# Second attention scores in two single PSUM banks, and layer 0's expert pieces only in turns with values

## The chip, the cores and the metric

The kernel runs on one core of a Trainium2 chip. The metric is the device time of one execution in microseconds (us); three runs of the kernel before are given by their median and their range. The profile is of one further execution of the same program on the chip.

The engines are named as in the profile: PE does the matmuls and PEld loads their weights, DVE is the vector engine, ACT the scalar engine (exponentials, ReLU, copies out of PSUM), POOL the third elementwise engine, SP the queue from which nearly all DMAs are issued. PSUM is the memory that matmuls write: here eight banks of 128 partitions by 512 numbers (fp32).

## What is computed

Two layers on a stream x of 16 batches by 512 tokens by 128. Each layer normalizes the stream and adds two branches to it.

```python
xn = layernorm(x)
x = x + L0_attn(xn)      # a memory trained chunk by chunk: 8 sequential steps
      + L0_ffn(xn)       # conv, 16-head attention (head size 8), then 8 dense experts 128 -> 512 -> 128
xn = layernorm(x)
x = x + L1_attn(xn)      # 16-head causal attention, conv, causal attention again with the same k and v
      + L1_ffn(xn)       # 32 sparse experts, the best 8 of each token
```

The attention is the usual one, softmax(q k / sqrt(8)) v, without a mask in layer 0 and causal in layer 1. The experts of layer 0 are computed for all tokens and weighted by softmax gates:

```python
h = relu(einsum("bsd,edf->bsef", x, w1) + b1)
y = einsum("bsef,efd->bsed", h, w2) + b2
moe_out = einsum("bse,bsed->bsd", probs, y)
```

## The kernel before

**Turns.** The work is cut into stages, each a Python generator. A class `Turns` (L273) runs them turn by turn: in each turn every live stage is resumed once, in the order of its priority, and issues the instructions up to its next `yield`. PE's order of instructions is exactly the order of issue (`ORDERED`, L634, and `manual_schedule`, L674); the other engines' orders come from a scheduler that is held to some of it (the `issue_after` lines of `Turns.run`). A matmul that waits holds up every later matmul. In a turn there stand, one after the other on PE:

- the first scores (`largest`, L374, priority 0): q by k for two heads side by side, one on each half of PE's rows, into two banks of the tag "bank". DVE takes the maximum of each row (L399; causal with the mask in one operation, L391, or with an addition ahead, L398). These maxima are later subtracted within the second scores.
- the second scores (`weighted`, L423, priority 1): k by q, the same scores transposed, into one tile of two banks (tag "p2", one buffer). ACT takes the exponential of both banks in one instruction (L470); in layer 1 POOL then clears what the causal mask forbids (L474).
- the values, in the same function (`tail`, L448, and `values`, L432): matmuls with 32 columns that sum exponentials times v into a bank of its own (tag "ctx"). They are issued right behind the second scores, in turns where enough heads wait: 4 in layer 0, 8 in layer 1. Such a turn puts "values" in `locks`, and the end of the turn takes it out.
- everything else (priority 3 and up): projections, transposes, the memory's steps, and last of all (priority 6) the experts of layer 0.

For causal attention a turn covers 512 or 384 columns of one head pair, 256 columns of two or 128 columns of four.

**Banks.** `work` (L177) gives a bank of the tag "bank", five in number. First scores, projections, transposes and experts share them. With the two of "p2" and the one of "ctx" that makes eight. `held` counts tiles that stay over a turn, and `room` and the experts' loop keep it under `pools["work"]` = 3.

**Experts.** `ffn` (L530) works through one batch: 64 pieces, 32 of `first` (`phe`: two matmuls of 128x512, then a ReLU on ACT at L584) and 32 of `second` (`pye`: eight matmuls of 128x128 at L594, which sum over four pieces in one held bank; after the fourth ACT scales it, L601, and POOL adds it up, L602). Pieces alternate first, second, first. The first pieces fetch the next expert's weights from DRAM (L516, L520). How many pieces a turn gets is decided at L613 to L619: `credit` grows each turn by 2750 ns less what the turn's other matmuls cost by the planner's own account (`load_ns`) and falls by 1000 a piece, and is never over 4000. From it comes `more`. With `pairs` set (it always is) `more` is rounded down to an even number, and in a turn with values it is 0 unless it is over 3. After that `look_ns`, an account of the time that DVE needs for the turn's maxima, may raise `more` where PE would otherwise be through too soon.

**Fillers.** Where no expert stage has run for two turns, `fill` (L198) adds a matmul whose result nobody reads, so that a turn has about 860 ns of full-array work.

**Stages in time.** Layer 0's attention and the memory's steps come first (to about 1640 us), layer 1's attention follows with the rest of layer 0's experts beside it (1640 to about 3050 us), then the end of layer 1 with its sparse experts.

Of the kernel before, what the change touches and what calls it, by code (L numbers as in the profile page):

```python
# [9 lines left out]
F32 = mybir.dt.float32  # L10
# [3 lines left out]
AF = mybir.ActivationFunctionType  # L14
# [3 lines left out]
P = 128  # L18
B, S, D = 16, 512, 128
# [18 lines left out]
SCALE = 1.0 / float(np.sqrt(DH))  # L38
# [44 lines left out]
def network(ctx: ExitStack, tc: tile.TileContext, a, out):  # L83
    nc = tc.nc
# [25 lines left out]
    def load(pool, name, shape):  # L110
        t = pool.tile(shape, F32, bufs=1, name="sb_" + name)
        nc.sync.dma_start(t, a[name])
        return t
# [26 lines left out]
    pools, done, locks, clock, newest, cleared, held, read, cell = {}, {}, set(), [0], [None], [None], [0], [0], []  # L140
# [11 lines left out]
    def acquire(name):  # L152
        while name in locks:
            yield
        locks.add(name)
# [12 lines left out]
    def hold(name):  # L168

        held[0] += 1  # L170
        return work(name)
# [3 lines left out]
        read[0] += 1  # L175

    def work(name):  # L177
        return pools["ps"].tile([P, 512], F32, tag="bank", bufs=5, name=name)

    def toks(ap):  # L180
        return ap.rearrange("p (t d) -> p t d", d=P)
# [4 lines left out]
    load_ns, look_ns, array_ns, at_ffn = [0.0], [0.0], [0.0], [-9]  # L186

    def mm(o, lhsT, rhs, start=True, stop=True):
        n = int(np.prod(rhs.shape[1:]))
        if lhsT.dtype == FR:  # L190
            load_ns[0] += 0.5 * (0.45 * n + 105)
        else:
            t = 0.42 * n if lhsT.shape[-1] == 32 and n >= P else 2 * max(0.834 * n, 110)
            load_ns[0] += t
            array_ns[0] += t
        nc.tensor.matmul(o, lhsT=lhsT, rhs=rhs, start=start, stop=stop)  # L196

    def fill():  # L198

        n = int((ARRAY - array_ns[0]) / 1.67) // P * P  # L200
        if clock[0] - at_ffn[0] > 2 and n > 0 and held[0] < pools["work"]:
            o = work("fill")
            nc.tensor.matmul(o[:, 0:n], lhsT=ident, rhs=cell[0][:, 0:n], start=True, stop=True)  # L203
        array_ns[0] = 0.0
# [39 lines left out]
    def turn4(src, name="tp"):  # L244

        tp = work(name)
        for t in range(4):
            nc.tensor.transpose(tp[:, t * P : (t + 1) * P], src(t), ident)  # L248
        load_ns[0] += 600
        array_ns[0] += 600  # L250
        return tp
# [13 lines left out]
    def ends(stage, name):  # L265
        yield from stage
        mark(*name)
# [87 lines left out]
    def widths(causal):  # L355

        for i in range(TB):
            n = S if not causal else S - i * P
            per = {S: 1, 3 * P: 1, 2 * P: 2, P: 4}[n]
            for t in range(0, NH, per):  # L360
                yield i, n, per, t
# [61 lines left out]
    def weighted(slot, vp, c, causal, cn, name):  # L423


        q, k, _ = slot
        yield from acquire("p2")
        cnv = cn.rearrange("p t (a c j d) -> p (t a) c j d", c=2, j=2, d=DH)
        old, last = [], []
        got = []  # L430

        def values(heads):  # L432
            for head in heads:
                kt, n, t, r, e = head
                lent.discard(id(head))
                g = 2 * (t % 2) + r
                j = t // 2
                mm(
                    got[0][32 * g : 32 * g + 32, S - n :], vp[:, kt, 4 * g + 2 * c + j, :], e,
                    start=(kt == 0 and j == 0), stop=(kt == TB - 1 and j == 1),  # L440
                )
            if kt == TB - 1 and t == NH - 1:
                cs = att.tile([P, S], F32, tag="cs", bufs=1, name="cs")
                nc.scalar.copy(cs, got[0])  # L444
                locks.remove("ctx")
                last.append(cs)

        def tail(least):  # L448
            if not got and "ctx" not in locks:
                locks.add("ctx")  # L450
                got.append(pools["ps"].tile([P, 512], F32, tag="ctx", bufs=1, name="pc"))
            if got and len(old) >= least:
                locks.add("values")
                for _ in range(min(len(old) // 4, 2)):
                    values([old.pop(0) for _ in range(4)])

        for i, (kt, n, per, t) in enumerate(widths(causal)):
            while len(old) >= pools["heads"] and not got and "ctx" in locks:
                yield
            s = pools["ps"].tile([P, 2, 512], F32, tag="p2", bufs=pools["p2"], name="s2")  # L460
            sv = s[:, :, 0 : per * n].rearrange("p r (i n) -> p r i n", i=per)
            for u in range(per):
                for r in range(2):
                    rr = slice(64 * r, 64 * r + 64)
                    mm(sv[:, r, u, :], k[rr, t + u, kt * P : (kt + 1) * P], q[rr, t + u, S - n :])
            tail(pools["heads"])

            pool = pools["weights"][i % len(pools["weights"])]
            e = pool.tile([P, 2, 512], F32, tag="e", bufs=3, name="e")
            nc.scalar.activation(e[:, :, 0 : per * n], s[:, :, 0 : per * n], AF.Exp, scale=SCALE)  # L470
            ev = e[:, :, 0 : per * n].rearrange("p r (i n) -> p r i n", i=per)
            if causal:
                for r in range(2):
                    cleared[0] = nc.gpsimd.affine_select(  # L474
                        out=ev[:, r, :, 0:P], in_=ev[:, r, :, 0:P], pattern=[[0, per], [1, P]],
                        compare_op=ALU.is_ge, fill=0.0, base=0, channel_multiplier=-1,
                    )
            for u in range(per):
                for r in range(2):
                    old.append((kt, n, t + u, r, ev[:, r, u, :]))  # L480
                    if pool is pools["mid"]:
                        lent.add(id(old[-1]))
            yield
        locks.remove("p2")
        free_slots.append(slot)
        turns.stages.append((turns.turn, 2, ends(summed(old, tail, last, c, cnv), name)))

    def summed(old, tail, last, c, cnv):

        while old:  # L490
            tail(4)
            yield
        cs, = last
        yield from room()
        held[0] += 1
        tp = turn4(lambda t: cs[:, t * P : (t + 1) * P], "tpc")
        yield
        tv = tp.rearrange("p (b j x) -> p b j x", j=2, x=16)
        rec = sm.tile([P, TB * NG, 2], F32, tag="rec", name="rec")
        nc.vector.reciprocal(rec, tv[:, :, :, DH])  # L500
        nc.vector.tensor_tensor(cnv[:, :, c], tv[:, :, :, 0:DH], bc(rec, 3, DH), ALU.mult)
        drop()
        yield
# [8 lines left out]
    credit, fetched = [0.0], {}  # L512
# [17 lines left out]
    def ffn(b):  # L530
# [44 lines left out]
        hs, pye, n = {}, [None], 4 * EXP0  # L575
# [34 lines left out]
        while at < len(units):  # L610

            at_ffn[0] = clock[0]
            credit[0] = min(credit[0] + TURN - load_ns[0], 4000)  # L613
            more = int(max(credit[0] + 500, 0) // 1000)
            if pools["pairs"]:
                more = more // 2 * 2 if "values" not in locks or more > 3 else 0
            if credit[0] > -2000:

                more = max(more, int((look_ns[0] - load_ns[0] - 400) / 1000 + 0.7))  # L619
            for fn, u in units[at : at + more]:  # L620

                if held[0] >= pools["work"] - (fn is second and u % 4 == 0):
                    break
                fn(u)
                at += 1
                credit[0] -= 1000
            next(gating, None)
            yield
# [10 lines left out]
    att = main.enter_context(tc.tile_pool(name="att", bufs=1))  # L639
# [1 line left out]
    fa = early.enter_context(tc.tile_pool(name="fa", bufs=2, side="right"))  # L641
    ff = main.enter_context(tc.tile_pool(name="ff", bufs=1))
    ps = main.enter_context(tc.tile_pool(name="psum", bufs=1, space=PSUM))
    pools.update(ps=ps, p2=1, work=3, weights=[att], mid=None, heads=4, pairs=True)
    Wt = Pack(load(fa, "pb", [P, sum(PB.values())]), PB)
    cell.append(Wt.t)
    row.update(load_rows(fa, "rows0", ROWS0))
# [447 lines left out]
    def back(layer, b, i, c):  # L1095
        yield from after(("tops", layer, b, i, c), lag=5)
        yield from after(("vals", layer, b))
        z = live[layer, b]
        if c == 0:
            z["cn"] = (l1 if layer else fa).tile([P, TB, D], F32, tag="cn", bufs=2, name="cn")  # L1100
        yield from weighted(z[i, c], z["vp"], c, layer == 1, z["cn"], ("back", layer, b, i, c))
# [31 lines left out]
    def experts0():  # L1133
        for b in range(B):
            yield from ffn(b)
# [27 lines left out]
        pass  # L1163
    for _ in padded_values(l1, 2):
        pass
    pools["pairs"] = True

    def middle(mid, b):

# [440 lines left out]
```

## Time and profile before

| | |
|---|---|
| median of three runs | 3685.94 us (3680.49 to 3687.93) |
| the profiled execution's own time | 3691.89 us |
| its span, first to last instruction | 3690.2 us |
| mean granted TensorE clock | 0.965 of full speed |
| instructions | 62824 |
| exponentials (L470) | 1216, 1191.9 us busy, 980 ns mean |
| expert matmuls `phe` / `pye` | 1024 / 4096, 539.8 / 564.6 us busy |
| causal masks on POOL (L474) | 1408, 469.6 us busy |
| fillers (L203) | 306 matmuls, 118.8 + 35.9 us busy |

How to read it: a row of the page's part 5 gives line, engine, operation, output<-input, form and count, then busy time and the mean of one, then the engine's idle time just before such instructions and what ended most of it. An fp32 matmul of the code is two PE instructions, so one `first` shows as two `phe` rows and one `second` as eight `pye` rows. Matmuls on the two halves of PE's rows run at the same time; so do four values matmuls on the four quarters of its columns. The granted clock over the run, in 40 slices of 92 us:

```profile
PE   6999999899999899999999999999999999998887
PEclk7999999899999999999999999999999999997888
```

PE is busy 90% or more of nearly every slice, and the clock dips at the start and in the last four slices.

### The profile page before, as it was taken

What the parts mean: (1) busy time and instruction counts of PE and PEld (TensorE: products, weight loads), DVE (VectorE), ACT (ScalarE), POOL (GpSimd) and SP (SyncE); (2) the same over time, 40 slices, a digit from 0 to 9 for tenths busy, and PEclk for the clock granted to TensorE, in tenths of its full rate; (3) what the DMA queues carried; (4) which work ended last, traced back from release to release, by engine and by line L of the source; (5) the groups of instructions that cost most, each with busy time, mean ns of one, the idle gap of its engine ahead of it and who ended that gap; (6) DMA issues with size and microseconds to landing.
All of it is one profiled execution on the core that took longest, in us unless ns stands there. A gap on an engine that the chain in (4) does not pass through costs nothing. (4 is left out here: it accounts for less than half of the span.)

```text
span 3690.2 us, 62824 instructions
## 1 busy us (share of the span) xinstructions
PE 3464.8 (94%) x22191; PEld 1928.6 (52%) x22191; DVE 2283.7 (62%) x5907; ACT 2156.5 (58%) x3703; POOL 1575.3 (43%) x2524
## 2 busy tenths in 40 slices
PE   6999999899999899999999999999999999998887
PEld 3445555454555455455555555555555655443443
DVE  5676656566756566556466666666666666777652
ACT  1556656665656687666566666666656665543433
POOL 5433532432441455432444344434443444433665
PEclk7999999899999999999999999999999999997888
DMA  5222222223123242443434443444344433333333
GB/s 171 68 68 74 74 76 72 68 72 85 55 67 94 85 114 88 129 124 104 136 95 134 114 133 99 125 117 133 96 130 125 119 101 110 106 103 94 83 86 90
DMA packets 290075, 370.83 MB, mean 100 GB/s; under 512 B 46017, under 2 KB 141409, under 8 KB 289377
## 3 DMA queue, kind: packets, MB, share of 16 engines
q1 hardware_dynamic: 282592, 359.99, 34.2%
q0 software_dynamic: 7168, 6.82, 1.1%
q8 instruction: 177, 2.90, 0.3%
q14 instruction: 138, 1.12, 0.1%
HBM read 236.85 MB, written 133.25 MB: 100 GB/s over the span
## 5 line engine op out<-in xcount | busy, mean ns | idle before, releaser
L470 ACT ACTIVATE e<-s 128x1024 f32<-128x1024 f32 (+1 forms) x1216 | 1191.9, 980 | 651.0 <-PE s L196 574.3
L399 DVE TENSOR_REDUCE nm<-s 128x1 f32<-128x512 f32 (+2 forms) x1408 | 906.5, 682 | 527.7 <-PE s L196 526.3
L391 DVE CUSTOM_DVE_ANT_0 s<-s,sb_const 128x512 f32<-128x512 f32 (+1 forms) x1024 | 624.2, 643 | 433.8 <-PE s L196 428.1
L474 POOL TENSOR_SCALAR_AFFINE_SELECT e<-e 128x128 f32<-128x128 f32 (+2 forms) x1408 | 469.6, 370 | 859.7 <-ACT e L470 852.9
L196 PE MATMUL s<-kx,qx 64*128 64x512 f32 (+3 forms) x3072 | 660.8, 433 | 59.3 <-DVE nm L399 15.3
L196 PE MATMUL pc<-e,vp 128*32 128x512 f32 (+3 forms) x6144 | 639.8, 508 | 30.6 <-POOL e L474 30.5
L196 PEld LDWEIGHTS s<-kx,qx 64*128 64x128 f32 x3072 | 295.1, 189 | 638.4 <-issue 254.6
L594 PEld LDWEIGHTS pye<-ew,hTe 128*128 128x128 f32 x4096 | 517.7, 192 | 173.9 <-issue 158.6
L196 PE MATMUL s<-qx,kx 64*128 64x512 f32 (+3 forms) x3072 | 535.1, 362 | 39.4 <-ACT e L470 28.3
L594 PE MATMUL pye<-ew,hTe 128*128 128x128 f32 x4096 | 564.6, 281 | 0.8 <-ACT hTe L584 0.8
L196 PE MATMUL phe<-x1T,ew 128*128 128x512 f32 x1024 | 539.8, 611 | 8.4 <-DVE nm L399 6.4
L584 ACT ACTIVATE hTe<-phe,sb_cols 128x512 f32<-128x512 f32 x512 | 353.1, 690 | 280.1 <-PE phe L196 278.0
L196 PEld LDWEIGHTS s<-qx,kx 64*128 64x128 f32 x3072 | 295.3, 190 | 85.1 <-ACT e L470 62.2
L602 POOL TENSOR_TENSOR ac<-ac,y 128x512 f32<-128x512 f32 x128 | 164.7, 1287 | 408.6 <-ACT y L601 380.7
L398 DVE TENSOR_TENSOR s<-s,sb_const 128x256 f32<-128x256 f32 (+1 forms) x384 | 180.9, 516 | 237.0 <-PE s L196 232.8
L196 PEld LDWEIGHTS pc<-e,vp 128*32 128x32 f32 x6144 | 154.3, 111 | 271.1 <-issue 177.4
L196 PEld LDWEIGHTS phe<-x1T,ew 128*128 128x128 f32 x1024 | 157.7, 192 | 59.8 <-issue 34.1
L601 ACT ACTIVATE y<-pye,pr 128x128 f32<-128x128 f32 x512 | 147.3, 369 | 30.8 <-PE pye L594 25.8
L391 DVE DVE_READ_ACCUMULATOR2_ANT nm<- 128x1 f32 x1024 | 144.5, 141 | 0.0
L203 PE MATMUL fill<-sb_pd,sb_const 128*128 128x512 f32 (+2 forms) x234 | 118.8, 595 | 0.2 <-DVE lo L330 0.2
L209 POOL TENSOR_SCALAR rs_t<-ss 128x4 f32<-128x4 f32 (+1 forms) x56 | 12.0, 214 | 239.6 <-ACT sq L262 238.4
L209 POOL TENSOR_SCALAR rs_t<-ln_mv 128x4 f32<-128x4 f32 x64 | 12.8, 200 | 178.3 <-DVE ln_mv L219 176.0
(294 smaller groups left out, 3898.8 us busy)
## 6 DMA issues: line engine op xcount, KB each, us to landing
ew<-in_ew SPq DMA_DIRECT2D x256, 256.0 KB
kx<-rk SPq DMA_DIRECT2D x192, 256.0 KB
qx<-rq SPq DMA_DIRECT2D x128, 256.0 KB
rq<-hi SPq DMA_DIRECT2D x64, 256.0 KB
rq<-lo SPq DMA_DIRECT2D x64, 256.0 KB
rk<-hi SPq DMA_DIRECT2D x64, 256.0 KB
rk<-lo SPq DMA_DIRECT2D x64, 256.0 KB
qx<-r SPq DMA_DIRECT2D x64, 256.0 KB
```

What stands on the lines that cost most here:

```text
L196: nc.tensor.matmul(o, lhsT=lhsT, rhs=rhs, start=start, stop=stop)
L203: nc.tensor.matmul(o[:, 0:n], lhsT=ident, rhs=cell[0][:, 0:n], start=True, stop=True)
L209: nc.gpsimd.tensor_scalar(t, src, scale, eps, ALU.mult, ALU.add)
L391: newest[0] = nc.vector.tensor_tensor_reduce(out=sv[r][:, 0, :], in0=sv[r][:, 0, :], in1=row["caus"][:, S - n :], scale=1.0, scalar=-BIG, ...
L398: nc.vector.tensor_tensor(dg, dg, bc(row["caus"][:, S - P :], 1, per), ALU.add)
L399: newest[0] = nc.vector.tensor_reduce(nm[:, qt, r, t : t + per], sv[r], AX.X, ALU.max)
L470: nc.scalar.activation(e[:, :, 0 : per * n], s[:, :, 0 : per * n], AF.Exp, scale=SCALE)
L474: cleared[0] = nc.gpsimd.affine_select(out=ev[:, r, :, 0:P], in_=ev[:, r, :, 0:P], pattern=[[0, per], [1, P]], compare_op=ALU.is_ge, fill= ...
L584: nc.scalar.activation(hs[i], ph, AF.Relu, bias=col("fb", i))
L594: nc.tensor.matmul(pye[0][:, t, :], lhsT=h[:, t * P : (t + 1) * P], rhs=w2[e][:, f, :], start=(f == 0 and t == 0), stop=(f == 3), skip_gro ...
L601: nc.scalar.mul(y[:, t, :], pye[0][:, t, :], pr[:, t, e : e + 1])
L602: nc.gpsimd.tensor_tensor(ac, ac, y, ALU.add)
```

## The change

Second scores take two single banks by `work`, from the tag that everything else uses; that tag now has seven buffers, and the tag "p2" is gone. The exponential becomes two instructions, one for each bank. The expert loop loses its rounding to pairs and the raising by `look_ns`: in a turn without values it issues no pieces unless `more` is 4; in a turn with values it issues `more` pieces, up to four since `credit` is capped at 4000.

```diff
@@ work
-        return pools["ps"].tile([P, 512], F32, tag="bank", bufs=5, name=name)
+        return pools["ps"].tile([P, 512], F32, tag="bank", bufs=7, name=name)
@@ weighted
-            s = pools["ps"].tile([P, 2, 512], F32, tag="p2", bufs=pools["p2"], name="s2")
-            sv = s[:, :, 0 : per * n].rearrange("p r (i n) -> p r i n", i=per)
+            s = [work("s2")[:, 0 : per * n] for r in range(2)]
+            sv = [x.rearrange("p (i n) -> p i n", i=per) for x in s]
             for u in range(per):
                 for r in range(2):
                     rr = slice(64 * r, 64 * r + 64)
-                    mm(sv[:, r, u, :], k[rr, t + u, kt * P : (kt + 1) * P], q[rr, t + u, S - n :])
+                    mm(sv[r][:, u, :], k[rr, t + u, kt * P : (kt + 1) * P], q[rr, t + u, S - n :])
             tail(pools["heads"])
...
-            nc.scalar.activation(e[:, :, 0 : per * n], s[:, :, 0 : per * n], AF.Exp, scale=SCALE)
+            for r in range(2):
+                nc.scalar.activation(e[:, r, 0 : per * n], s[r], AF.Exp, scale=SCALE)
@@ ffn
             more = int(max(credit[0] + 500, 0) // 1000)
-            if pools["pairs"]:
-                more = more // 2 * 2 if "values" not in locks or more > 3 else 0
-            if credit[0] > -2000:
-
-                more = max(more, int((look_ns[0] - load_ns[0] - 400) / 1000 + 0.7))
+            if "values" not in locks and more < 4:
+                more = 0
@@ set-up
-    pools.update(ps=ps, p2=1, work=3, weights=[att], mid=None, heads=4, pairs=True)
+    pools.update(ps=ps, work=3, weights=[att], mid=None, heads=4)
@@ before layer 1
-    pools["pairs"] = True
```

## The prediction

> **What bounds the kernel now.** I read the page first (parts 1 and 5), then the waits, then the busy time by stretch, then the timeline of the middle stretch. From the page:
>
> ```profile
> PE 3464.8 (94%) x22191; PEld 1928.6 (52%) x22191; DVE 2283.7 (62%) x5907; ACT 2156.5 (58%) x3703; POOL 1575.3 (43%) x2524
> ...
> L196 PE MATMUL s<-qx,kx 64*128 64x512 f32 (+3 forms) x3072 | 535.1, 362 | 39.4 <-ACT e L470 28.3 <-DMA qx<-top 9.6
> ```
>
> PE is busy 94%, no other engine over 62%. The second line is the second scores (`s<-qx,kx`; the first scores are `s<-kx,qx`). Their wait for the exponential that frees the one two-bank buffer is 28.3 us in all. A busy PE is not yet a PE at its peak, so I asked how dense it is. Busy time by stretch, of which the middle one holds layer 1 with the experts:
>
> ```profile
> 0.00:1640.00 1640.00, 1522.56 (x8666) 823.17 (x8666) 1014.02 (x1978) 1001.04 (x1920) 666.11 (x673) 0.96 0.30 88
> 1640.00:3050.00 1410.00, 1386.47 (x9952) 825.67 (x9951) 866.38 (x2685) 872.41 (x1398) 590.63 (x1239) 1.00 0.41 117
> 3050.00:3690.00 640.00, 555.76 (x3577) 279.76 (x3575) 403.29 (x1245) 283.02 (x385) 318.53 (x612) 0.89 0.37 96
> ```
>
> (time, then PE, PEld, DVE, ACT, POOL, granted clock.) In the middle PE has 23 us idle in 1410. PE's timeline there shows the regular turn:
>
> ```profile
> 2205.14 0.50 PE L196 MATMUL s<-kx,qx 64*128 64x512 f32 x2
> 2205.48 0.34 PE L196 MATMUL s<-qx,kx 64*128 64x384 f32 x2
> 2205.74 1.16 PE L594 MATMUL pye<-ew,hTe 128*128 128x128 f32 x8
> 2206.74 1.02 PE L196 MATMUL phe<-x1T,ew 128*128 128x512 f32 x2
> 2207.69 0.50 PE L196 MATMUL s<-kx,qx 64*128 64x512 f32 x2
> ```
>
> Scores, two expert pieces, scores again: each starts as soon as the one before is through. The two pieces (1.95 us) stand between one turn's second scores and the next turn's, so the exponential (1.02 us) is always done. Start to start over the whole trace, PE's excess over the usual pitch of each step is about 380 us, but only 85 of it in the middle stretch. **PE in its written order is the bound; what adds a wait to PE adds time.**
>
> **What the change does to the order.** The planner takes 1279 turns in both kernels, and every stage falls in the same turn but for the experts (layer 0's last expert ends in turn 1082 instead of 1059). What moves is where the 1024 pieces stand. Before: 331 turns carry two pieces, mostly turns without values. After: 277 turns with values carry one to four, 75 others mostly four. The built PE order then has 232 places where two turns' scores follow each other with nothing between (65 in layer 0, 167 in layer 1); before it has 14. This is the heart of the forecast. The trace has the 14, and their price. One of them:
>
> ```profile
> 2020.94 0.51 PE L196 MATMUL s<-kx,qx 64*128 64x512 f32 x2
> 2021.28 0.34 PE L196 MATMUL s<-qx,kx 64*128 64x384 f32 x2
> 2021.45 0.40 PE L196 MATMUL s<-kx,qx 64*128 64x512 f32 x2
> 2021.66 0.81 ACT L470 ACTIVATE e<-s 128x768 f32<-128x768 f32 x1 [0.34 <-PE s L196]
> 2021.77 0.67 DVE L391 CUSTOM_DVE_ANT_0 s<-s,sb_const 128x512 f32<-128x512 f32 x1
> 2022.36 0.14 DVE L391 DVE_READ_ACCUMULATOR2_ANT nm<- 128x1 f32 x1
> 2022.52 0.44 PE L196 MATMUL s<-qx,kx 64*128 64x384 f32 x2 [0.67 <-ACT e L470]
> ```
>
> Second scores could have started at about 2021.79 (0.34 after the first); they start 0.73 later, when the exponential has ended. Thirteen of the 14 waits lie between 0.27 and 1.21 us; the seven in layer 1 are 0.83 on average.
>
> **Cost of the 232 places with the new buffers.** Bare scores take four banks a turn, two turns eight; there are seven, and one of them mostly holds `pye`. In the built order the following second scores take, in the commonest case, the banks of the *preceding turn's* first score (freed by DVE's maximum) and first second score (freed by the first half exponential). So they still wait for the turn before. From t=0 at the first scores, rows above: second scores at 0.34, next first scores 0.51, next second scores could start at 0.85. DVE starts 0.53 after its scores (2205.14 to 2205.67) and needs 0.69+0.14: free at 1.36. ACT: the exponential's group, split by form, gives 1025 ns at 1024 columns and 813 at 768, 0.83 ns a column, so 128x512 takes about 600; it starts 0.38 after its scores, or after the last piece's ReLU (0.69 us, till 0.86): free at 1.37 to 1.5. The wait is 0.5 to 0.65 us; I take 0.6. Bounds: 0.3 if DVE and ACT are always idle and another bank is free, 0.85 as today. 232 x 0.6 = 139 us, less the 14 x 0.83 = 12 that exist: **+127**.
>
> **Values after bare scores.** 48 layer-0 places go straight to values that need the turn before's second half exponential: done at 0.86+2x0.6=2.07, values else start near 1.85; 48 x 0.25 = 12. In layer 1 (119 places) POOL's mask (0.29 each) must follow; the first half of the values covers it unless POOL is in one of its 1.28 us additions: 0 to 0.3 us each, I take 0.1: 12. **+24**. Of these 151 us some shortens later waits (stretch 0:1640 has 11% excess, the middle 6%): I pass on 85%, **+128**.
>
> **Exponentials in halves.** 1216 become 2432; 2x600-1025 and 2x492-813 are both +172 ns: ACT gets +209 us, 58% to 64%. Hidden by ACT's idle time (651 us before this group alone), save in the places counted. Here the Trainium skill (Perfetto Trace Analysis, Optimizing Scalar/DVE Operations) cuts both ways: grouping operations helps a saturated engine, and an unsaturated one that makes bubbles elsewhere should be broken up. By the second the split should pay; but the row has only 28.3 us of such bubbles, 12 of them counted above. I credit the other 16, **-16**; at most the 88 us that lie between first and second scores in all.
>
> **Fewer changes of shape.** A change from 64-row scores or 32-column values to full 128x128 matmuls and back costs PE: eight `pye` matmuls take 995 ns after scores and 891 in a chain, `phe` 962 against 861, and the step to scores adds 93. The order has 958 such round trips instead of 1061: 103 x 0.197 = **-20**. Fillers (L203): 153 to 141, at 0.53: **-6**. 24 pieces leave turns 600 to 1059 for turns 1059 to 1083, where there is slack: 24 x 0.97 = 23, less 5: **-18**. The experts' weight loads move with the pieces on SP's queue, past rows and tops loads by a few turns; no engine waits on them today, cost 0, at most 10.
>
> **Sum.** +128-16-20-6-18 = +68 on the profiled execution's 3691.9 us (span 3690.2). That lies 6 above the median 3685.9, so **3754 us**, +1.8%.
>
> **Rivals.**
> *The added banks win (faster).* Everything turns on the wait per bare place. Savings are 60 us; passed-on cost is 0.85x(232w-12)+20. At w near 0.25 both are equal; at 0.1, with 20 more saved at score waits, it is 3686+10+20-80 = 3636; between these, 3640 to 3678. For it: ACT and DVE have idle time and the skill asks that matmul groups rotate through banks (same page, Optimizing Tensor Performance, Matmuls). Against: by that rule the row could give 28 us, and the order shows bare places going back to the same banks. 0.17.
> *Nothing (doesn't do what it says).* 1051 of the 2432 second-score tiles take a bank whose last user was a second score, usually of the turn before; if the pieces' move is neutral as well, 3686. 0.08.
> *The clock falls.* After 3120 us, in turns without experts, sixteen `pc` matmuls take 3.19 us against 1.92 at 2203, clock 0.92. The skill (TensorE: Matmul & The Clock Gate, Part 1) says that the clock halves after an idle window of about 3.4 us; this trace shows the lower clock only where the experts have ended. A bare turn with its wait is about 2 us, so by the rule the clock holds; if the middle still went to 0.97, 1410 x 0.03 = 42 more: 3796, and with w at 0.85 as well, 3845. 0.15, the main case 0.60.
>
> **How the numbers follow.** Measurement can tell about 0.2% (7 us). Faster 0.17, within 0.2% 0.08, slower 0.75. The likeliest case's own range is w from 0.35 to 0.8, 3705 to 3795. For eight in ten I reach into the faster case and over the clock case: 3665 to 3840.
>
> **What would show it.** Right: PE's wait for ACT `e` and DVE `nm` in front of score matmuls grows from about 45 to over 120 us; PE's busy share in the middle falls to 93% or less; turns 600 to 1059 take 40 to 80 us more; the exponential row has 2432 at about 570 ns. Wrong: second scores after bare turns start within 0.2 us of the first scores' end; or the waits grow as said and the span doesn't, which would mean that PE's order was not the bound; or the half exponential is far from 600 ns.

## The result, and the profile after

| | before | after |
|---|---|---|
| median (range) of four runs each | 3686.93 us (3680.49 to 3692.67) | 3834.76 us (3832.34 to 3837.18) |
| span of the profiled execution | 3690.2 us | 3830.6 us |
| mean granted clock | 0.965 | 0.964 |
| `phe` / `pye` pieces, instructions on PE | 1024, 22191 | 1024, 22167 |

The changed kernel takes 1.0399 times as long, interval 1.0382 to 1.0416. Below, every difference in us of a kernel is its ratio less one, times 3687: here +147.

From the page of the changed kernel, its engines, the exponentials, the first scores (`s<-kx,qx`) and the second scores (`s<-qx,kx`), and last the first scores' row of the kernel before:

```profile
PE 3560.8 (93%) x22167; PEld 1996.2 (52%) x22167; DVE 2265.0 (59%) x5907; ACT 2218.9 (58%) x4919; POOL 1593.4 (42%) x2524
...
L471 ACT ACTIVATE e<-s 128x512 f32<-128x512 f32 (+1 forms) x2432 | 1270.9, 577 | 522.7 <-PE s L196 464.7
...
L196 PE MATMUL s<-kx,qx 64*128 64x512 f32 (+3 forms) x3072 | 662.9, 421 | 54.3 <-DVE nm L399 16.4
...
L196 PE MATMUL s<-qx,kx 64*128 64x512 f32 (+3 forms) x3072 | 614.6, 374 | 75.8 <-DVE nm L391 32.7
...
L196 PE MATMUL s<-kx,qx 64*128 64x512 f32 (+3 forms) x3072 | 660.8, 433 | 59.3 <-DVE nm L399 15.3
```

PE does the same work but for 12 fillers less, and is busy 96 us longer. The reason is that a group of scores can wait halfway through and still count as busy. Its two halves, one for each bank, usually start together (0.003 us apart in the median of both traces); when the second half's bank is late, the halves run one after the other, and the profile counts both as work. The row that grew is the second scores': 535.1 busy and 39.4 idle before, 614.6 and 75.8 now, +116 us in all. The first scores' row hardly moved, because changes cancel in it: measured from the start of one half to the start of the other, the first scores wait 79 us in all before, 74 of them away from bare places; in the changed kernel they wait 94, of which 67 at bare places. (A bare place is one where two turns' scores follow each other on PE with nothing between.) What PE waits for by name, in the order of the answer (total, times, longest):

```profile
PE s L196 <- DVE nm L391: 39.0, 80, 6.7
PE s L196 <- DVE nm L399: 35.6, 69, 5.0
...
PE s L196 <- ACT e L471: 18.7, 33, 2.0
```

Before it was 28.3 for the exponential and 15.3 for L399. The exponential's share has fallen and DVE's row maxima (L391, L399, `nm`) have taken its place. Busy time by stretch, columns as before:

```profile
0.00:1640.00 1640.00, 1533.08 (x8544) 837.83 (x8544) 1005.16 (x1947) 1012.43 (x2388) 658.95 (x663) 0.97 0.29 86
1640.00:3050.00 1410.00, 1338.39 (x9096) 795.10 (x9095) 785.66 (x2488) 822.12 (x1729) 555.74 (x1137) 0.98 0.38 109
```

In the first 1640 us PE issued 8544 matmuls instead of 8666; in the middle stretch 9096 instead of 9952. So most of the loss lies in layer 1 beside the experts. Matching the two traces turn by turn (a turn is counted here by its scores, 1216 in all) says the same: the changed kernel is 30 us behind at turn 512, where layer 0's scores end, 44 at turn 600, 103 at 900, 152 at 1050, and then loses nothing more (136 at 1215).

**One bare place.** The usual turn of before had second scores 0.34 us after first scores and the next first scores after pieces. Here is a place of the changed kernel where two turns' scores stand together (PE only):

```profile
2536.47 0.50 PE L196 MATMUL s<-kx,qx 64*128 64x512 f32 x2
2536.81 0.34 PE L196 MATMUL s<-qx,kx 64*128 64x384 f32 x2
2536.98 0.34 PE L196 MATMUL s<-kx,qx 64*128 64x384 f32 x2
2537.91 0.50 PE L196 MATMUL s<-qx,kx 64*128 64x256 f32 x4 [0.59 <-DVE nm L391]
```

The last line could have started about 0.3 after the third, at 2537.3, and starts 0.6 later: a bank of the first line is free only when DVE has read it. That is the wait that the forecast had priced. But other places look like this one, of the dearest kind (all engines, some lines left out):

```profile
2586.95 0.61 PE L196 MATMUL s<-qx,kx 64*128 64x512 f32 x2
...
2587.47 1.29 DVE L398 TENSOR_TENSOR s<-s,sb_const 128x512 f32<-128x512 f32 x2
2587.49 1.08 ACT L471 ACTIVATE e<-s 128x512 f32<-128x512 f32 x2 [0.59 <-PE s L196]
...
2587.65 0.98 PE L196 MATMUL s<-kx,qx 64*128 64x512 f32 x2
2588.14 0.18 PEld L196 LDWEIGHTS s<-kx,qx 64*128 64x128 f32 x1 [0.34 <-ACT e L471]
...
2588.62 0.45 PE L196 MATMUL s<-qx,kx 64*128 64x384 f32 x1
...
2588.66 1.28 DVE L399 TENSOR_REDUCE nm<-s 128x4 f32<-128x512 f32 x2
...
2589.49 0.47 PE L196 MATMUL s<-qx,kx 64*128 64x384 f32 x1 [0.42 <-DVE nm L399]
```

Four waits in one place. The first scores of 2587.65 come 0.70 after the second scores before them, where 0.23 is usual. Their own second half starts only at 2588.14, 0.49 late, when an exponential has ended (the line of PEld), and the row shows one group of 0.98 us instead of 0.50. The second scores follow 0.97 after the first instead of 0.34, the 0.49 included. And their second half, in the other of the two single banks, comes another 0.87 later, with DVE's maxima named as what it waited for. The profile gives only 0.42 of all this as idle.

### The profile page after: what moved, and what is told of

Its sections match the earlier page's. It is cut to its first block, busy times and chain, and to the rows that moved or that the text cites. A ratio compares the mean times of both kernels' runs of the same rounds, so it can differ in the third digit from the quotient of the medians.

```text
span 3830.6 us, 64164 instructions
## 1 busy us (share of the span) xinstructions
PE 3560.8 (93%) x22167; PEld 1996.2 (52%) x22167; DVE 2265.0 (59%) x5907; ACT 2218.9 (58%) x4919; POOL 1593.4 (42%) x2524
## 5 line engine op out<-in xcount | busy, mean ns | idle before, releaser
L471 ACT ACTIVATE e<-s 128x512 f32<-128x512 f32 (+1 forms) x2432 | 1270.9, 577 | 522.7 <-PE s L196 464.7
L399 DVE TENSOR_REDUCE nm<-s 128x1 f32<-128x512 f32 (+2 forms) x1408 | 905.7, 683 | 553.5 <-PE s L196 552.8
L391 DVE CUSTOM_DVE_ANT_0 s<-s,sb_const 128x512 f32<-128x512 f32 (+1 forms) x1024 | 620.2, 645 | 625.2 <-PE s L196 592.2
L475 POOL TENSOR_SCALAR_AFFINE_SELECT e<-e 128x128 f32<-128x128 f32 (+2 forms) x1408 | 485.1, 369 | 866.1 <-ACT e L471 842.2
L196 PE MATMUL pc<-e,vp 128*32 128x512 f32 (+3 forms) x6144 | 669.0, 517 | 36.2 <-POOL e L475 32.1
L196 PE MATMUL s<-qx,kx 64*128 64x512 f32 (+3 forms) x3072 | 614.6, 374 | 75.8 <-DVE nm L391 32.7
L595 PEld LDWEIGHTS pye<-ew,hTe 128*128 128x128 f32 x4096 | 528.7, 194 | 231.4 <-issue 203.3
L196 PEld LDWEIGHTS s<-kx,qx 64*128 64x128 f32 x3072 | 304.5, 187 | 523.7 <-issue 219.0
L196 PEld LDWEIGHTS s<-qx,kx 64*128 64x128 f32 x3072 | 332.1, 188 | 193.9 <-DVE nm L391 59.1
L391 DVE DVE_READ_ACCUMULATOR2_ANT nm<- 128x1 f32 x1024 | 145.4, 142 | 0.0
L203 PE MATMUL fill<-sb_pd,sb_const 128*128 128x512 f32 (+2 forms) x210 | 104.0, 582 | 1.3 <-ACT e L471 0.6
```

The source lines that it names most:

```text
L391: newest[0] = nc.vector.tensor_tensor_reduce(out=sv[r][:, 0, :], in0=sv[r][:, 0, :], in1=row["caus"][:, S - n :], scale=1.0, scalar=-BIG, ...
L399: newest[0] = nc.vector.tensor_reduce(nm[:, qt, r, t : t + per], sv[r], AX.X, ALU.max)
L471: nc.scalar.activation(e[:, r, 0 : per * n], s[r], AF.Exp, scale=SCALE)
L475: cleared[0] = nc.gpsimd.affine_select(out=ev[:, r, :, 0:P], in_=ev[:, r, :, 0:P], pattern=[[0, per], [1, P]], compare_op=ALU.is_ge, fill= ...
L595: nc.tensor.matmul(pye[0][:, t, :], lhsT=h[:, t * P : (t + 1) * P], rhs=w2[e][:, f, :], start=(f == 0 and t == 0), stop=(f == 3), skip_gro ...
```

## The experiments

Four theories were on the table. **W**: PE waits for banks at the 232 bare places that the new piece rule makes. **H**: the halved exponential or the shared tag costs. **P**: long chains of pieces behind values cost. **V**: values right after bare scores wait for POOL's causal mask. Each run's ratio is to a kernel before on the same chip.

### The two halves apart

**e1_banks_only**: seven banks and half exponentials, with the piece rule of before (cut from the changed kernel).

```diff
-            if "values" not in locks and more < 4:
-                more = 0
+            if pools["pairs"]:
+                more = more // 2 * 2 if "values" not in locks or more > 3 else 0
+            if credit[0] > -2000:
+                more = max(more, int((look_ns[0] - load_ns[0] - 400) / 1000 + 0.7))
```

> Seven shared banks and halved exponentials, with the old rule for the experts' pieces: PE's order has 14 bare places (two turns' scores with nothing between), as before. Theory W (the loss of 148 us is PE's waiting at the 232 bare places that the new rule makes): 3670 to 3700 us, since the halves' extra ACT time is hidden and the score waits of the old order are at most some 20 us. Rival H (the loss comes from the halves and from second scores competing in the shared tag): 3780 to 3830.

Measured: 3651.0 us (3645.93 to 3653.62), ratio 0.9894 [0.9878, 0.9911], -39 us, below the range expected. It is the fastest version that keeps all the work, ahead of both kernels. Its first and second scores, from the page:

```profile
L196 PE MATMUL s<-kx,qx 64*128 64x512 f32 (+3 forms) x3072 | 624.6, 431 | 43.9 <-ACT e L471 15.4
L196 PE MATMUL s<-qx,kx 64*128 64x512 f32 (+3 forms) x3072 | 534.2, 357 | 28.1 <-DMA qx<-top 9.0
```

No wait for the exponential leads the second scores' row any more, but that row gained only 12 us (535.1 busy and 39.4 idle before). More of the gain lies in the first scores: 36 us less busy (660.8 before) and 15 less idle. Their halves start 30 us apart in all, instead of 79. H falls for the whole of this half.

**e2_rule_only**: the new piece rule on the kernel before (five banks, the two-bank tile, one exponential).

```diff
-            if pools["pairs"]:
-                more = more // 2 * 2 if "values" not in locks or more > 3 else 0
-            if credit[0] > -2000:
-                more = max(more, int((look_ns[0] - load_ns[0] - 400) / 1000 + 0.7))
+            if "values" not in locks and more < 4:
+                more = 0
```

> The new rule for the pieces with the old banks (five shared, one two-bank buffer for second scores, one exponential per turn): 232 bare places. Theory W: each waits for a whole exponential, 0.8 to 1.1 us, so 3830 to 3900 us, no better than with the changed banks. Rival H: 3690 to 3720.

Measured: 3948.7 us (3945.14 to 3952.28), ratio 1.0709 [1.0691, 1.0727], +261 us, above the range that W gave. PE's first wait:

```profile
PE s L196 <- ACT e L470: 168.1, 229, 3.5
```

229 waits for the exponential, where before had 37. By their times 184 of them lie at bare places, and 227 of 233 such places in the trace hold some idle time of PE: the two-bank tile is the one released by the exponential, and the rule sends PE back to it at once. The rule costs 261, the banks alone bring 39, and together they cost 147: at bare places the banks are worth more than elsewhere.

**e7_halves_only**: the kernel before, with the exponential of the two-bank tile in two instructions.

```diff
-            nc.scalar.activation(e[:, :, 0 : per * n], s[:, :, 0 : per * n], AF.Exp, scale=SCALE)
+            for r in range(2):
+                nc.scalar.activation(e[:, r, 0 : per * n], s[:, r, 0 : per * n], AF.Exp, scale=SCALE)
```

> The kernel before with each exponential in two instructions on the same two-bank tile; banks and piece rule as before. If the halves' extra ACT time is hidden and the 37 us that seven banks with halves gained come from the banks: 3685 to 3705 us. If the halves bring the gain (values and masks of the first half start sooner): 3650 to 3670.

Measured: 3688.83 us (3675.85 to 3700.22), ratio 0.9998 [0.9982, 1.0014]: nothing. So the 39 us of e1 are the banks' (that the halves are needed for them is not excluded: single banks with one whole exponential were not tried).

### How much a piece between the scores is worth

**e3_one_piece**: the changed kernel, but a turn that would be bare (`load_ns` under 1000) gets one piece if `more` has one.

```diff
             if "values" not in locks and more < 4:
-                more = 0
+                more = min(more, 1) if load_ns[0] < 1000 else 0
```

> The changed kernel, but a turn whose other matmuls are accounted under 1000 ns gets one piece: 20 bare places instead of 232, and 1180 changes of matmul shape and back instead of 958. Theory W: nearly all waits go; the changes of shape cost 119 x 0.197 = 23 us more than before the change: 3685 to 3730. Rival P (it is long chains of pieces behind values that delay later stages, not the bare places): 3780 or more, since values turns keep up to four pieces.

Measured: 3704.55 us (3700.94 to 3707.26), ratio 1.0041 [1.0027, 1.0055], +15 us. One piece of about 1 us in those turns leaves 20 bare places of 232 and takes back 132 of 147 us. But it also shortens the chains: turns with three or four pieces behind values fall from 172 to 71. So e3 alone leaves P open; e10 below keeps the whole order and decides against it as a main cause.

**e8_no_look** and **e9_any_turn** take e1 and change the old rule: e8 drops the raising by `look_ns`, e9 also allows pairs in any turn, with values or without.

```diff
# e8 (from e1)
-            if credit[0] > -2000:
-                more = max(more, int((look_ns[0] - load_ns[0] - 400) / 1000 + 0.7))
# e9 (from e8)
-                more = more // 2 * 2 if "values" not in locks or more > 3 else 0
+                more = more // 2 * 2
```

> Seven shared banks and halves, with the old rule for pairs but without the raising by the account of DVE's time: 25 bare places, 213 with values alone between, and 1015 changes of matmul shape and back against 1061. Theory W (bare places cost about 1 us each, a change of shape and back 0.2): 11 more bare places against 46 fewer changes, so within 15 us of the 3651 of the same banks with the whole rule. If finer filling of turns is what made the old rule good: 3680 or more.

> Seven shared banks and halves, pieces in pairs in any turn, whether it has values or not, and without the raising by DVE's time: 29 bare places, 122 with values alone, 1103 changes of shape and back. Theory W: 15 bare places and 42 changes more than the best so far (3651): 3665 to 3690 us. If it is the place behind values that costs, as rival P has it, 3720 or more.

Measured: e8 3652.6 us (3647.92 to 3658.38), ratio 0.9913 [0.9885, 0.994], -32; e9 3667.46 us (3659.3 to 3671.25), ratio 0.9943 [0.9925, 0.9961], -21. Their orders have 25 and 29 bare places. The removed `look_ns` is no cause of the loss, and pieces in turns with values, in pairs, cost some 11 us at most.

### What PE waits for at a bare place

**e5_no_mask_after** and **e6_no_mask_before** leave out POOL's causal mask, in the changed kernel and in the one before. The edit is the same in both.

```diff
-            if causal:
+            if False:
```

> The changed kernel without POOL's causal masks in layer 1 (its attention is then not causal). Values then wait for the exponential alone. Theory V (a good part of the loss is values that wait for mask and exponential of the bare turn just before): 3770 to 3800 us, 35 to 65 less than with masks. If the score banks alone make the loss: within 12 us of 3835.

> The kernel before without POOL's causal masks in layer 1 (attention not causal), as the measure for the run above. Two pieces stand between a turn's exponentials and the values that use them, so both theories expect 3672 to 3690 us: at most 15 less.

Measured: e5 3817.04 us (3811.59 to 3823.52), ratio 1.035 [1.0322, 1.0378]; e6 3667.11 us (3662.12 to 3671.92), ratio 0.9946 [0.9922, 0.9969]. The masks are worth 18 us in the one and 20 in the other, so the difference of 147 stays: V falls, as far as it rests on the mask. (Both lie below what was expected if banks alone make the loss, by some 5 us.)

**e10_no_max_after** and **e11_no_max_before** leave out DVE's row maxima in layer 1 and the additions of the mask that go with them (a constant stands in their place), again in the changed kernel and in the one before.

```diff
+        if causal:
+            newest[0] = nc.vector.memset(nm, 1.0)
...
-            for r in range(2):
+            for r in range(0 if causal else 2):
```

> The changed kernel without DVE's row maxima in layer 1 (constants in their place, so layer 1's attention is wrong there): the first scores' banks are free as soon as they are written. If DVE's maxima set half or more of the waits at bare places: 3835 falls by 60 to 110, to 3725 to 3775. If the exponentials set them: by 10 to 40, to 3795 to 3825.

> The kernel before without DVE's row maxima in layer 1 (constants in their place), as the measure for the run above. PE is the bound and waits little for DVE: 3655 to 3685 us.

Measured: e10 3682.89 us (3680.65 to 3696.05), ratio 0.9992 [0.9979, 1.0006], -3; e11 3644.88 us (3637.85 to 3648.84), ratio 0.9876 [0.9851, 0.9901], -46, both below every range expected. Without the maxima the change costs 43 us instead of 147: 104 of the 147 need DVE's maxima in layer 1. The order of PE is that of the changed kernel, with all its bare places, and the middle stretch of e10 has

```profile
1640.00:3050.00 1410.00, 1370.85 (x9853) 833.38 (x9853) 182.02 (x803) 869.18 (x1874) 601.10 (x1239) 0.99 0.41 117
```

9853 matmuls in the same 1410 us, against 9096 with the maxima and 9952 in the kernel before. A bare place of e10 (PE only, next to each other):

```profile
2400.17 0.45 PE L196 MATMUL s<-kx,qx 64*128 64x384 f32 x2
...
2400.45 0.39 PE L196 MATMUL s<-qx,kx 64*128 64x512 f32 x2
...
2400.68 0.40 PE L196 MATMUL s<-kx,qx 64*128 64x256 f32 x4
...
2400.92 0.40 PE L196 MATMUL s<-qx,kx 64*128 64x512 f32 x2
```

Four groups at 0.28, 0.23 and 0.24 us from each other: no wait. Without DVE's work on the scores, a bare place of layer 1 costs about 0.2 us beyond the usual, and the long chains behind values, which are all still there, cost little as well (P). The edit does two things at once: it frees the first scores' banks, and it takes most of DVE's load (182 us in this stretch instead of 786). That the banks are what counts is not shown by this run alone; for it speaks that in the changed kernel 67 of PE's 84 us of idle time at bare places end with a maximum in `nm`.

### How many banks

**e4_six_banks** is the changed kernel with six buffers in the shared tag, **e12_six_old_rule** is e1 with six.

```diff
-        return pools["ps"].tile([P, 512], F32, tag="bank", bufs=7, name=name)
+        return pools["ps"].tile([P, 512], F32, tag="bank", bufs=6, name=name)
```

> The changed kernel with six buffers in the shared tag, one bank left unused. If the waits at bare places are for banks (theory W as first put: eight score tiles in seven banks), each of 232 places waits for one tile more, 0.3 to 0.6 us: 3900 to 3970. If they wait because DVE and ACT need their time for two turns of scores whatever the banks, within 15 us of 3835.

> Halves and a shared tag of six buffers with the old piece rule (14 bare places). With the new rule the sixth instead of the seventh bank cost 201 us. If banks run out chiefly because bare turns ask for eight tiles in a row, the loss here is small: 3655 to 3700 us, against 3651 with seven. If six are too few anywhere: 3750 or more.

Measured: e4 4036.14 us (4032.15 to 4040.99), ratio 1.0939 [1.0921, 1.0958], +346, above both ranges; e12 3797.34 us (3790.77 to 3801.72), ratio 1.0291 [1.0274, 1.0309], +107. In e4 the waits move where W says: first scores after second scores, 31 us beyond the usual at bare places of the changed kernel, cost 89 in e4. But e12, with 14 bare places as before, loses 146 against e1, where 3655 to 3700 us were expected. PE's waits of e12:

```profile
PE pc L196 <- POOL e L475: 28.7, 23, 4.6
PE s L196 <- ACT e L471: 22.4, 21, 9.0
PE s L196 <- ACT hTe L585: 13.6, 21, 7.5
PE s L196 <- DVE nm L399: 13.5, 24, 1.6
...
PE phe L196 <- ACT e L471: 12.8, 23, 0.7
```

Now scores wait for an expert's ReLU and an expert's first piece for an exponential: with six, every turn is short of a bank, not only the bare ones. The seventh bank is worth 146 us with the old rule and 199 with the new. That number alone does not separate bare places from the rest; e12 shows that it mostly isn't about them. Which of the shared tag's users runs short first in e12 was not tried further.

## Why the prediction was right in direction and too small

Forecast +68, measured on the spans +140. Splitting PE's time start to start, the usual pitches of all steps in the order sum to 3286 us before and 3250 after, -36; what lies beyond them is 381 before and 557 after, +176. Together +140, the change of the span. The forecast had -44 (shape changes 20, fillers 6, displaced pieces 18) and +112 (+128 and -16). **The part that it got wrong is the waits, by 64 us.** The measured 3835 lies outside the likeliest case's own range (3705 to 3795). It lies inside the wide one (3665 to 3840) only because that reached over the case of a lower clock, which did not come about as a whole: luck.

- *232 bare places decide.* Right. The trace of after has them (233 by the same count), e2 has one wait for each, and e3 takes most of the loss away by filling them.
- *The price per place, w = 0.6, at most 0.85 "as today".* This is the step that failed. Measured from the second scores to what follows the next second scores, beyond usual pitches, a place costs 1.02 us on average (median 0.73, a tenth over 1.87). Its parts: 0.13 ahead of the first scores, 0.50 from their start to the start of the second, 0.39 behind that, of which about 0.30 lies inside the second scores between their two banks. The forecast priced only the middle part, and for what lies behind it 0.1 to 0.25 us for values. The middle part's size came out nearly right (0.5 to 0.65 against 0.50), but partly by luck: about 0.29 of it lies inside the first scores, between their two banks, and only the rest is the wait ahead of the second scores that the forecast meant. It left out that two single banks come free at two different times, so that one group of matmuls can wait twice, and that the next first scores need banks too.
- *The calibration, 0.83 at the old places.* It had the same gap: the 14 old places cost 0.83 in that one step but 1.35 in all. Nor was the time of release safe: DVE was taken as free at 1.36 after the first scores, which fits the first of the two maxima; a bare pair has four, at 0.65 to 0.84 us each, one after the other, and narrow scores need additions too: the first turn of the second place above keeps DVE for about 2.5 us. That class (first scores of 128 columns, second of 512, then a turn of 512 and 384) is the dearest, 1.74 on average (37 places). With the maxima gone in layer 1 the mean falls to 0.41, about 0.2 in layer 1 and 1.0 in layer 0.
- *Values after bare scores, +24.* The half of it for POOL's mask fell with V in e5 and e6. The other half, layer 0's values that wait for an exponential, was not tested apart; what passes between the second scores' last matmul and what follows them is about 0.1 us a place. 
- *85% passed on.* In size about right: the bare places add 233 x 1.02 less 19 for the old ones, 219; all waits together grew by 176, 80%.
- *Credit -16 for the banks.* Too small: e1 gives -39. The credit was read from the second scores' idle time (28.3 us), and most of the gain lay in another row: the first scores', as work of a busy PE (36 us) and as idle time (15).
- *Exponentials in halves, hidden.* Right (e7). The lengths were right too, 600 ns at 512 columns and 491 at 384, but ACT's load rose by 62 us, not 209. (With 600 ns the first of the two differences is 175 ns, not 172; nothing hangs on it.)
- *Shape changes, fillers, displacement.* -36 in place of -44. The 24 displaced pieces' share can't be seen alone; in turns 1000 to 1050 the changed kernel loses 18 us more, so the slack assumed there is doubtful.
- *The clock* stayed over the whole run: 0.964. In the middle stretch it went from 1.00 to 0.98: the trace has it granted at half there in twelve periods of 3.4 or 6.8 us, 55 us in all, against one of 3.4 before. That costs at most 27 us, so this rival came true in part; one period begins at 2589.7, right behind the second place above, though the profile gives PE only 0.42 us of idle time in the 3.4 us before it. The stretches ahead of 1640 and behind 3050 lost less than before (111 us by the same sum, against 130), so over the whole the clock explains at most 7 us of the difference. That the lower clock follows the waits is likely (e10, with the same order, has 0.99) but not shown. The forecast's reading that the lower clock stands only where the experts have ended was wrong: its own table has 0.96 in the first 1640 us.
- *The signs.* Turns 600 to 1059 take 108 us more, not 40 to 80. PE's named waits for the exponential and the maxima ahead of scores went from 44 to 93 us, not over 120, and PE's busy share in the middle is 94.9%, not 93 or less, though more time was lost than forecast. Both were set on idle time, which sees a wait inside a group as work.
- *The rival that the added banks win.* They do win, by themselves: e1 is the faster kernel that it described. Its condition, w below 0.25, was met only in layer 1 of e10, where DVE does not hold the banks.

In total, 219 at bare places, less 39 for the banks elsewhere, 20 for shape and 6 for fillers is 154, against +147. The agreement is no proof of each term: those four are not independent (e1 and e2 don't add up).

## What to carry to other kernels

Where matmul groups write buffers that another engine reads, the work that stands between two groups is their cover: before moving it, count the places left with none, and price each by every buffer that the next groups need and by when its reader is really through, one reader after the other. Price it from start to start, not from idle time: a group that waits halfway shows as busy. And test the halves of a combined change apart: here one was worth -39 us, the other cost 261.

## What the runs showed of the hardware

- The row of the halved exponential has 2432 x 577 ns, 1403 us, in 1270.9 us busy: two that follow each other overlap. A pair takes 1.08 us (`x2` above), one whole exponential 1.025. ACT's busy time as a whole rose by 62.4 us for 1216 more instructions, 51 ns each, and that of the exponentials alone by 79.0 (from 1191.9), 65 ns each, where the durations alone say 172. The Trainium skill (Perfetto Trace Analysis, Optimizing Scalar/DVE Operations) gives about 51 ns for a ScalarE instruction on PSUM and says that the profiled latency is about twice the overhead because half of it overlaps with the next instruction. The forecast added up durations; an estimate by that section, 1216 x 51 ns, comes to 62, as the whole engine shows; the exponentials' own row is somewhat above it.
- With eight banks, one for the context and seven shared, giving up one cost 146 to 199 us of 3650 to 3835, more than any other single edit that left the piece rule alone.
- A busy row can hold a wait: the second scores' busy time grew from 535.1 to 614.6 us with the same 3072 matmuls, and went back to 534.2 in e1. The first scores' went the other way, from 660.8 to 624.6 in e1. Two halves of a group that run one after the other (0.98 us above) count as work, though together they take 0.50.
